# A decoder layer on one core: evacuations of PSUM and experts' ReLUs go to the engine that the kernel's own planner has free first

## The chip, the core and the metric

The kernel runs on one core of a Trainium2 chip. A core has TensorE (PE, matrix multiplications into PSUM), VectorE (DVE), ScalarE (ACT), GpSimd (POOL) and SyncE (SP, which here issues the DMA transfers). The metric is the device time of one execution in microseconds, given as the median of several runs. One more execution was profiled; its own time stands beside its span below.

## The reference, cut to what matters

A decoder layer over 16 sequences of 512 positions with 256 channels, in fp32. Each of three parts is added to its input and normalized.

```python
# 1. linear attention, 16 heads of 16 channels, two key and value sets
q = x + x @ Wq + bq;  ks[k] = x + x @ Wk[k] + bk[k];  vs[k] = x + x @ Wv[k] + bv[k]
state = prod_k( einsum('bhnd,bhne->bhde', ks[k] / 32, vs[k] / 32) )
x = norm(x + (norm(q @ state) * ln_g + ln_b) @ Wo + bo)
# 2. cross-attention to 64 context rows per sequence, 16 heads of 64
sim = (x @ Wq.T) . (ctx @ Wk.T) * 64**-0.5, masked;  attn = softmax(sim)
x = norm(x + (attn @ v) @ Wout.T + b_out)
# 3. mixture of 8 experts, each taking the first 1024 tokens with a positive weight
w = softmax(x @ router_w.T + router_b)
x = norm(x + sum_e w[:, e] * relu(x @ experts_inter[e]) @ experts_out[e])   # for the tokens taken
```

The router's weights are positive, so each expert takes the first 1024 tokens, which are the first two sequences (the "head"). A loop at the end of the program covers other cases; with these inputs it runs no pass.

## The kernel before

**Tiles and stages.** Rows of a sequence lie in four tiles of 128 (t = 0 to 3). Every result of TensorE goes into one of eight PSUM banks (`bank`, tag "ps", 128 x 512 fp32) and from there, through VectorE or ScalarE, to SBUF. The linear attention is folded: `gram` forms x^T x of a sequence (ps_g, ps_gt), `self_attention` multiplies it by the key and value weights (ps_gk, ps_s), builds a 256 x 256 matrix m (ps_m, ps_b) and applies it (ps_o), normalizes (z), transposes (ps_zt) and applies Wo (ps_p). The setup transposes the context and its weights (`context_keys`, `transposed`: tiles cn, nat to cT, wT), multiplies them (`context_rows`: ps_kv into st or stk) and, in `context_values`, multiplies the values by Wout (ps_vo into the four vst buffers) and stores them to DRAM (vo_dram), from where each sequence loads its vo tiles (six buffers). `router_columns`, `router_weights` and `output_weights` have small matmuls of 8 columns (L404 ps_rw, L537 ps_wo).

`cross_attention` forms the similarities of one row tile in two halves (ps_sim, L814); VectorE takes the maximum (mx, L820) and subtracts it (s, L821), ScalarE takes the exponential (L822). `softmax` then sums (sm, L800), inverts (L801), multiplies on GpSimd (L802) and transposes on VectorE into pT (L804). After the fourth row tile ps_x (L834, 256 records of 32 rows) multiplies pT and vo, and VectorE adds the result to x1 (L841). `routing` computes the expert weights (w_all) of a sequence. `experts` multiplies the head by an expert's first weights (ps_h, L946), takes the ReLU of each 128 x 256 piece into hT (L952 on ScalarE for odd f, L954 on VectorE for even f) and multiplies by the second (ps_e, L963; result added on VectorE, L970). `ranks` (L891 to L919) computes how many tokens come first for each expert, and `last_norm` writes the head out (y).

**Who evacuates.** `evac` (L186 on ScalarE, L188 on VectorE) copies a bank to SBUF, taking the two engines in turn through `flip`. It serves cT, wT, xT, st, stk, vst, g and xwoutT. Other evacuations have a fixed engine.

**What sets the order.** The program is written as six generators (streams): grams, context, self-attention, cross-attention, routing and experts. `weave` traces them step by step: it takes, of the streams that are ready at the planner's TensorE clock, the one that is least far in its plan (`Stream.time`), and lets it run to its next `yield`. A class `Model` follows the traced instructions with durations of its own: it holds when each engine is free (`free`), when each tile was made and last used, the end of the step (`end`) and TensorE's time in it (`took`). `yield WAIT` makes a stream ready only at the modelled end of its step, and `until(lambda: made(...))` polls until the model has a tile ready; in front of ps_x it polls for pT and vo. `beside` starts a further stream (each `softmax`, the loads of vo, each `last_norm`) that is ready at `model.end`. `in_order` then fixes the traced order on TensorE, VectorE, ScalarE and GpSimd; SP's transfers keep an order that the framework derives. So a change in the model's times changes the order on every engine.

Of the kernel before, what the change touches and what calls it, by code (L numbers as in the profile page):

```python
# [27 lines left out]
class Model:  # L28
# [2 lines left out]
    WIDE = {"PE": 0.25, "DVE": 0.15, "Activation": 0.15, "Pool": 0.15}  # L31

    def __init__(self, nc):
        self.nc, self.free, self.dma = nc, {}, 0.0
        self.made, self.used, self.slots, self.rows, self.seen = {}, {}, {}, P, 0

    def tile(self, name, key, bufs):
# [28 lines left out]
    def run(self):  # L66

        traced = self.nc.cur_bb.bb.instructions
        end = now = self.free.get("PE", 0.0)
        self.took = 0.0  # L70
        for ins in traced[self.seen:]:
            kind, engine = type(ins).__name__, str(ins.engine).split(".")[-1]
            aps = [[a.bass_ap for a in l if hasattr(a, "bass_ap")] for l in (ins.ins, ins.outs)]
            names = [[a.name for a in l] for l in aps]
            at = 0.0
            for made, used, l in ((1, 0, names[0]), (1, 1, names[1])):
                for n in l:
                    if kind == "InstDMACopy" and self.made.get(n, (0, 0))[1] == "SP":
                        continue
                    for known, book in ((made, self.made), (used, self.used)):  # L80
                        if known and n in book:
                            t, by = book[n]
                            at = max(at, t + (self.WIDE.get(by, 0.0) if by != engine else 0.0))
            if kind == "InstDMACopy":
                size = 4 * min(a.size() for l in aps for a in l)
                start = max(at, self.dma if now < 40 else 0.0)
                self.dma = start + size / 220e3
                done = self.dma + 2.0
            elif names[1]:
                start = max(at, self.free.get(engine, 0.0))  # L90
                done = self.free[engine] = start + self.duration(ins, kind, engine)
                if engine == "PE":
                    self.took += done - start
                else:
                    end = max(end, done + 0.15)
            else:
                continue
            for n in names[0] + names[1]:
                self.used[n] = max(self.used.get(n, (0.0, None)), (done, engine), key=lambda p: p[0])
            for n in names[1]:  # L100
                self.made[n] = (done, engine)
        self.seen, self.end = len(traced), end
        return end
# [13 lines left out]
def decoder_layer(  # L117
# [25 lines left out]
    nc = tc.nc  # L143
# [23 lines left out]
    model = Model(nc)  # L167
# [9 lines left out]
    def bank(name):  # L177
        return psp.tile([P, 512], FP, tag="ps", name=name)

    flip = [0]  # L180

    def evac(dst, src):

        flip[0] ^= 1
        if flip[0]:
            nc.scalar.copy(dst, src)  # L186
        else:
            nc.vector.tensor_copy(dst, src)  # L188
# [83 lines left out]
    with ExitStack() as att:  # L272
# [649 lines left out]
        def last_norm(b, t):  # L922
            y = wk1.tile([P, C], FP, tag=("z", "xt")[t % 2], name="y")
            yield WAIT
            yield from normalized(y.unsqueeze(1), lambda _: x2_head[:, b, t, :C], 1)
            yield WAIT
            nc.sync.dma_start(out=out[b, t * P:(t + 1) * P, :], in_=y)

        def experts():

            wi = wo_ = None
            yield from until(lambda: 0 in head_T and made(head_T[0]))
            for e in range(E):
                if e == 0:
                    wi = load_inter(e)
                    wo_ = load_outer(e)
                for n in range(CAP // TB):
                    b, t0 = divmod(n * TB // P, NT)  # L940
                    yield from until(lambda: b in head_T and made(head_T[b]))
                    hT = []
                    for f in range(NF):
                        ps = bank("ps_h")
                        for cc in range(NC):
                            nc.tensor.matmul(  # L946
                                ps[:, :TB], wi[:, cc, f * P:(f + 1) * P],
                                head_T[b][:, cc, t0 * P:t0 * P + TB], start=(cc == 0), stop=(cc == NC - 1),
                            )
                        h = ffn.tile([P, TB], FP, tag="hT", name="hT", bufs=12)  # L950
                        if f % 2:
                            nc.scalar.activation(h, ps[:, :TB], AF.Relu)  # L952
                        else:
                            nc.vector.tensor_relu(h, ps[:, :TB])  # L954
                        hT.append(h)
                        yield
                    if n == CAP // TB - 1 and e + 1 < E:
                        wi = load_inter(e + 1)
                    yield from until(lambda: finished["routing"] > b)
                    for t in range(TB // P):  # L960
                        ps = bank("ps_e")
                        for f in range(NF):
                            nc.tensor.matmul(  # L963
                                ps[:, :C], hT[f][:, t * P:(t + 1) * P], wo_[:, f, :],
                                start=(f == 0), stop=(f == NF - 1),
                            )
                            if f % 4 == 3:
                                yield
                        acc = x2_head[:, b, t0 + t, :C]
                        nc.vector.scalar_tensor_tensor(  # L970
                            acc, ps[:, :C], w_all[:, b * NT + t0 + t, e:e + 1], acc, ALU.mult, ALU.add
                        )
                        if e == E - 1:
                            beside(experts_st, last_norm(b, t0 + t))
                    if n == CAP // TB - 1 and e + 1 < E:
                        wo_ = load_outer(e + 1)

        def load_inter(e):
            t = ffn.tile([P, NC, FF], FP, tag="wi", name="wi", bufs=1)
            nc.sync.dma_start(out=t, in_=w_inter[e].rearrange("(c p) f -> p c f", p=P))  # L980
            return t

        def load_outer(e):
            t = ffn.tile([P, NF, C], FP, tag="wo_", name="wo_", bufs=1)
            nc.sync.dma_start(out=t, in_=w_out[e].rearrange("(f p) c -> p f c", p=P))
            return t
# [17 lines left out]
        def beside(st, gen):  # L1004

            new = Stream(gen).plan(st.time(), 0.0, 1.0)
            new.ready = model.end
            streams.append(new)

        def weave():  # L1010
            model.run()
            while streams:
                clock = model.free["PE"] = model.free.get("PE", 0.0)
                now = [st for st in streams if st.ready <= clock]
                if not now:
                    model.free["PE"] = min(st.ready for st in streams)
                    continue
                st = min(now, key=Stream.time)
                wait = next(st.gen, "end")
                st.end = max(st.end, model.run())  # L1020
                st.spent += model.took
                if wait == "end":
                    streams.remove(st)
                elif wait == WAIT:
                    st.ready = st.end
                else:
                    st.ready = clock + (wait or 0.0)
# [18 lines left out]
        def made(*tiles):  # L1046
            return all(model.made[t.name][0] <= model.free["PE"] for t in tiles)

        def until(ready):
            while not ready():  # L1050
                yield 0.5
# [63 lines left out]
        self_st, cross_st = Stream(all_self_attention()), Stream(all_cross_attention())  # L1115
        routing_st = Stream(all_routing()).plan(SETUP + STEP, STEP, 1.0)
        experts_st = Stream(experts()).plan(SETUP + 1.3 * STEP, (B - 0.1) * STEP, FFN)
        self_st.plan(0.0, SETUP, 16.5)
        cross_st.plan(SETUP, STEP, 28.0)
        traced = nc.cur_bb.bb.instructions  # L1120
        first = len(traced)
        streams += [grams_st, context_st, self_st, cross_st, routing_st, experts_st]
        weave()
        in_order(traced[first:])

# [86 lines left out]
```

## Time and profile before

| | |
|---|---|
| median of 3 runs | 1387.06 us (1386.35 to 1387.56) |
| the profiled execution: own time | 1389.4 us |
| the profiled execution: span | 1387.6 us |
| granted TensorE clock, mean | 0.994 |
| busy: TensorE, VectorE, ScalarE, GpSimd | 1365.9, 850.7, 402.2, 203.7 us |

The span runs from the first to the last instruction of the core; the execution's own time lies around it. Busy times are sums over instructions. In a row of a group, "x128" is the count, then come the busy time, the mean of one in ns, and the time that the engine stood idle before it with what ended that (the releaser). PEclk is the share of full speed that TensorE's clock was granted. A matmul in fp32 leaves two records, a transpose two; "ps_x x256" is one sequence.

### The profile page before, as it was taken

The numbers are of one execution on the slowest core, as the hardware profiler recorded it, in microseconds if no ns is written. First come the engines' busy times: TensorE is split into PE (matmuls) and PEld (weight loads), VectorE is DVE, ScalarE is ACT, GpSimd is POOL, SyncE is SP. The second block draws the span as 40 slices with busy tenths as digits, with TensorE's granted clock in tenths as the row PEclk, the third lists the DMA queues.
The fourth block names the chain that finished last, engine by engine and source line by source line (L and its number), as shares of the span: only waits on it lengthen the run. The fifth ranks groups of instructions, "written<-read, shape, count | busy, mean of one in ns | idle before, by whom it ended". The sixth has DMA issues, their size and how long they took to land.

```text
span 1387.6 us, 24209 instructions
## 1 busy us (share of the span) xinstructions
PE 1365.9 (98%) x9630; PEld 1077.9 (78%) x9630; DVE 850.7 (61%) x1957; ACT 402.2 (29%) x912; POOL 203.7 (15%) x140
## 2 busy tenths in 40 slices
PE   8999999999999999999999999999999999999997
PEld 5766576877878787878878787878888787878686
DVE  2445848466584848475584848475665939484744
ACT  1134224132232314142233323142323323232322
POOL 0001112112020111112020112112020202111200
PEclk9999999999999999999999999999999999999999
DMA  8657775511515153522606053513334061505211
GB/s 260 203 136 191 189 195 163 142 32 42 145 53 150 46 142 106 127 77 52 181 24 164 31 142 106 126 62 77 110 95 123 16 187 46 147 26 126 91 56 40
DMA packets 98372, 153.57 MB, mean 111 GB/s; under 512 B 15560, under 2 KB 70096, under 8 KB 98256
## 3 DMA queue, kind: packets, MB, share of 16 engines
q1 hardware_dynamic: 98256, 151.98, 40.1%
q8 instruction: 78, 1.28, 0.4%
q14 instruction: 38, 0.31, 0.1%
HBM read 114.71 MB, written 37.22 MB: 109 GB/s over the span
## 4 chain that ended last, share of the span: by engine, by line
PE 89%; DVE 5%; DMA 2%; SPq 1%; ACT 1%; issue 1%; ACTq 0%; DVEq 0%
PE ps_x L834 16%; PE ps_sim L814 15%; PE ps_e L963 15%; PE ps_h L946 15%; PE ps_gk L629 4%; PE ps_p L711 4%; PE ps_o L687 3%; PE ps_kv L437 3%; PE ps_t L233 2%; PE ps_kq L751 2%; PE ps_vo L492 2%; PE ps_s L641 2%; PE ps_g L555 2%; PE ps_zt L700 1%; PE ps_m L670 1%; PE ps_g L560 1%
## 5 line engine op out<-in xcount | busy, mean ns | idle before, releaser
L946 PE MATMUL ps_h<-head_T,wi 128*128 128x256 f32 x1024 | 239.1, 379 | 0.0
L834 PE MATMUL ps_x<-vo,pT 32*128 32x264 f32 x4096 | 234.9, 384 | 3.9 <-DVE pT L804 3.7
L814 PE MATMUL ps_sim<-kq,x1T 128*128 128x512 f32 x512 | 235.0, 593 | 0.0
L834 PEld LDWEIGHTS ps_x<-vo,pT 32*128 32x128 f32 x4096 | 211.5, 186 | 26.1 <-issue 5.6
L946 PEld LDWEIGHTS ps_h<-head_T,wi 128*128 128x128 f32 x1024 | 193.4, 190 | 38.8 <-issue 13.0
L802 POOL TENSOR_TENSOR s<-s,sm 128x1024 f32<-128x1024 f32 x64 | 121.7, 1901 | 539.8 <-DVE sm L801 501.4
L841 DVE TENSOR_TENSOR x<-ps_x,x 128x264 f32<-128x264 f32 x64 | 23.2, 426 | 226.3 <-PE ps_x L834 226.3
L822 ACT ACTIVATE s<-s 128x512 f32<-128x512 f32 x128 | 80.7, 630 | 276.1 <-DVE s L821 276.0
L814 PEld LDWEIGHTS ps_sim<-kq,x1T 128*128 128x128 f32 x512 | 94.5, 190 | 83.2 <-issue 74.5
L820 DVE TENSOR_REDUCE mx<-ps_sim 128x8 f32<-128x512 f32 x128 | 86.1, 673 | 42.0 <-PE ps_sim L814 41.6
L821 DVE TENSOR_TENSOR s<-ps_sim,mx 128x512 f32<-128x512 f32 x128 | 88.5, 692 | 4.4
L725 POOL TENSOR_TENSOR x<-x,bout 128x1056 f32<-128x1056 f32 x16 | 38.7, 2420 | 320.7 <-ACT hT L952 172.6
L804 DVE STREAM_TRANSPOSE pT<-s 128x1024 f32<-128x1024 f32 x64 | 78.6, 1228 | 7.0 <-POOL s L802 7.0
L952 ACT ACTIVATE hT<-ps_h 128x256 f32<-128x256 f32 x128 | 46.9, 376 | 119.9 <-PE ps_h L946 119.8
L701 ACT ACTIVATE zT<-ps_zt,shift,gain 128x512 f32<-128x512 f32 x32 | 23.2, 775 | 189.5 <-PE ps_zt L700 189.5
L800 DVE TENSOR_REDUCE sm<-s 128x16 f32<-128x1024 f32 x64 | 77.1, 1204 | 0.4 <-ACT s L822 0.4
L261 ACT ACTIVATE rstd<-bn_mv,eps 128x4 f32<-128x4 f32 (+1 forms) x70 | 20.7, 295 | 159.5 <-DVE bn_mv L250 156.0
L267 ACT ACTIVATE x<-x,off,rstd 128x264 f32<-128x264 f32 (+1 forms) x112 | 58.3, 591 | 29.3 <-DVE off L265 29.3
L687 PE MATMUL ps_o<-m,xT 128*128 128x264 f32 x256 | 66.7, 387 | 0.0
L954 DVE TENSOR_SCALAR hT<-ps_h 128x256 f32<-128x256 f32 x128 | 52.2, 409 | 22.5 <-PE ps_h L946 22.3
L711 PE MATMUL ps_p<-wo,zT 128*128 128x264 f32 x256 | 63.1, 387 | 0.0
L629 PE MATMUL ps_gk<-wk,g 128*128 128x256 f32 x256 | 61.2, 382 | 0.0
(174 smaller groups left out, 1897.4 us busy)
## 6 DMA issues: line engine op xcount, KB each, us to landing
vo<-vo_dram SPq DMA_DIRECT2D x512, 132.0 KB, 4.2
vo_dram<-vst SPq DMA_DIRECT2D x128, 132.0 KB, 2.4
xt<-in_x_dram SPq DMA_DIRECT2D x16, 512.0 KB, 4.0
wi<-L_ffn_experts_inter_dram SPq DMA_DIRECT2D x8, 1024.0 KB, 5.3
gx<-in_x_dram SPq DMA_DIRECT2D x15, 512.0 KB, 4.2
x_rest<-x SPq DMA_DIRECT2D x14, 512.0 KB, 3.1
out_dram<-x SPq DMA_DIRECT2D x14, 512.0 KB, 2.9
kT<-k_dram SPq DMA_DIRECT2D x8, 512.0 KB, 3.3
```

Of the source, the lines that this page charges most:

```text
L629: nc.tensor.matmul(ps[:, :C], blk, wk[:, j, k, :], start=(j == 0), stop=(j == NC - 1))
L687: nc.tensor.matmul(ps[:, :CX], xT[:, cc, t * P:(t + 1) * P], m[:, cc, :], start=(cc == 0), stop=(cc == NC - 1))
L711: nc.tensor.matmul(ps[:, :CX], zT[:, cc, t * P:(t + 1) * P], wo[:, cc, :], start=(cc == 0), stop=(cc == NC - 1))
L802: nc.gpsimd.tensor_mul(s, s, sm.unsqueeze(2).to_broadcast([P, NH, J]))
L804: nc.vector.transpose(probsT[:, :, t, :], s.rearrange("p h (a j) -> p (h a) j", a=2))
L814: nc.tensor.matmul(ps, x1T[:, cc, t * P:(t + 1) * P], kq[:, cc, hf * 512:(hf + 1) * 512], start=(cc == 0), stop=(cc == NC - 1),)
L820: nc.vector.tensor_reduce(mx[:, hs], sim, AX.X, ALU.max)
L821: nc.vector.tensor_sub(s[:, hs, :], sim, mx[:, hs].unsqueeze(2).to_broadcast([P, 8, J]))
L822: nc.scalar.activation(s[:, hs, :], s[:, hs, :], AF.Exp, scale=SCALE)
L834: nc.tensor.matmul(ps[q][:, :CX], probsT[pq, blk].rearrange("p t i -> p (t i)"), vos[c][pq, i, :], start=(c == 0 and i == 0), stop=(c == 7 ...
L946: nc.tensor.matmul(ps[:, :TB], wi[:, cc, f * P:(f + 1) * P], head_T[b][:, cc, t0 * P:t0 * P + TB], start=(cc == 0), stop=(cc == NC - 1),)
L963: nc.tensor.matmul(ps[:, :C], hT[f][:, t * P:(t + 1) * P], wo_[:, f, :], start=(f == 0), stop=(f == NF - 1),)
```

## The change

`evac` and the ReLUs of `experts` no longer take turns. A new function `scalar_first` first lets the model follow what has been traced so far, then takes ScalarE if the model has it free no later than VectorE, where a time before TensorE's own clock counts as TensorE's clock. If both are free by then, ScalarE is taken. Since the model now runs in the middle of a step too, `took` and `end` are collected over a step and set to zero before each step in `weave`; before, each call of `run` began anew. With that `model.end` is zero when `beside` is called at the beginning of a step, where it used to be the end of the step traced before.

```diff
@@ class Model
-        self.nc, self.free, self.dma = nc, {}, 0.0
+        self.nc, self.free, self.dma, self.took, self.end = nc, {}, 0.0, 0.0, 0.0
@@ Model.run
-        end = now = self.free.get("PE", 0.0)
-        self.took = 0.0
+        now = self.free.get("PE", 0.0)
+        end = max(self.end, now)
@@ decoder_layer
-    flip = [0]
+    def scalar_first():
+
+
+        model.run()
+        pe, dve, act = (model.free.get(e, 0.0) for e in ("PE", "DVE", "Activation"))
+        return max(act, pe) <= max(dve, pe)
 
     def evac(dst, src):
 
-        flip[0] ^= 1
-        if flip[0]:
+        if scalar_first():
             nc.scalar.copy(dst, src)
         else:
             nc.vector.tensor_copy(dst, src)
@@ experts
-                        if f % 2:
+                        if scalar_first():
                             nc.scalar.activation(h, ps[:, :TB], AF.Relu)
                         else:
                             nc.vector.tensor_relu(h, ps[:, :TB])
@@ weave
                 st = min(now, key=Stream.time)
+                model.took = model.end = 0.0
                 wait = next(st.gen, "end")
```

## The prediction

> **What bounds the kernel now.** I read the page's busy times first, then its chain, then TensorE's waits, then the timeline at each place where TensorE stands.
>
> ```profile
> span 1387.6 us, 24209 instructions
> PE 1365.9 (98%) x9630; PEld 1077.9 (78%) x9630; DVE 850.7 (61%) x1957; ACT 402.2 (29%) x912; POOL 203.7 (15%) x140
> PEclk9999999999999999999999999999999999999999
> PE 89%; DVE 5%; DMA 2%; SPq 1%; ACT 1%; issue 1%; ACTq 0%; DVEq 0%
> ```
>
> TensorE (PE) is the bound: busy for 98%, and 89% of the chain. Both orders hold the same 5461 TensorE instructions, so its work is fixed. What can be won is where it stands (1387.6 - 1365.9 = 21.7 us) or runs slowly; what can be lost is a new stop. VectorE (DVE) at 61% and ScalarE (ACT) at 29% matter only where one of them ends last in front of TensorE. Those places:
>
> ```profile
> PE ps_x L834 <- DVE pT L804: 3.7, 2, 3.2
> PE ps_t L233 <- DMA nat<-in_L_xattn_Wkv_dram: 2.4, 1, 2.4
> PE ps_e L963 <- DVE hT L954: 1.8, 1, 1.8
> PE ps_vo L492 <- DVE u L570: 0.8, 1, 0.8
> PE ps_vo L492 <- ACT st L186: 0.7, 1, 0.7
> ```
>
> Columns: us in total, times, longest. Between 349 and 1349 us TensorE stands for hardly anything (156.00 of 156.00 us busy in each stretch but one): nothing is to be won there. The open places are the start, the setup up to 193 us, two ps_x (192 to 349 us) and the tail.
>
> The clock has its own cost. Windows of 3.4 us, last columns PEclk, DMA share, GB/s:
>
> ```profile
> 15.50:18.90 3.40, 3.40 (x16) 3.17 (x15) 1.02 (x2) 0.58 (x1) 0.10 (x1) 0.50 0.79 277
> 66.70:70.10 3.40, 3.40 (x15) 3.21 (x15) 2.18 (x3) 0.00 (x0) 0.00 (x0) 0.50 0.00 0
> 70.10:73.50 3.40, 3.40 (x12) 2.75 (x12) 0.00 (x0) 0.00 (x0) 0.00 (x0) 0.50 0.00 0
> 336.30:339.70 3.40, 2.88 (x28) 2.56 (x32) 0.37 (x1) 0.00 (x0) 1.54 (x1) 0.50 0.02 5
> ```
>
> Half speed for one window costs 1.7 us of work. Two windows follow an idle gap (13 to 15 us, 333.6 to 336.8 us); two follow no gap at all.
>
> **The change part by part.** The instruction orders of both programs show what moves. 37 operations go from VectorE to ScalarE: 20 ReLUs, 8 xT, 10 st, 6 stk, 2 cT, a wT and an xwoutT leave VectorE, while 3 vst and a net 8 g pieces come to it. At the means of the groups (ReLU 409 against 376 ns, a 128x512 copy 683 to 692 against 574 to 595) VectorE loses about 25 us of 850.7, ScalarE gains about 22 us of 402.2. Neither is the bound, so this alone is worth nothing. More comes from the planner: it resets model.end before each step, so a softmax put beside the cross-attention is ready at once, where before it waited for the end of the step before. Between the second subtraction (L821) and the row sum (L800) stood mostly 5 to 11 VectorE instructions; now mostly 2 to 5. The whole TensorE order shifts with it.
>
> *1. Start: +1.85 us.*
>
> ```profile
> 9.81 1.04 PE L233 MATMUL ps_t<-ident,cn 128*128 128x128 f32 x8
> 10.69 0.27 PE L573 MATMUL ps_gt<-ident,g 128*128 128x128 f32 x1
> 10.79 1.91 PE L555 MATMUL ps_g<-gx 128*128 128x257 f32 x8
> 15.12 1.70 PE L233 MATMUL ps_t<-ident,nat 128*128 128x128 f32 x8 [2.42 <-DMA nat<-in_L_xattn_Wkv_dram]
> ```
>
> Before, ps_gt and the second sequence's ps_g fill the wait for nat. Now the transposes of nat stand ahead of both (all four cT copies go to ScalarE, and ps_gt waits for g behind them). The load is the eleventh row of SP's queue in both orders, so it lands at about 15.1 us as before. TensorE then stands from 10.7 on, and 0.11 + 1.74 us (8 at 0.2175, the steady pace of ps_g) are done later. The half-speed window is there already. Ends: 0 if nat lands earlier, +1.85; I take +1.85.
>
> *2. Clock at 63 to 74 us: -0.9.* The row first: PEclk is 0.50 from 66.7 to 73.5 us though TensorE never stands; what it did before was 16 matmuls of 8 columns (1.7 us), 8 transposes, and more 8-column ones. The Trainium skill, "TensorE: Matmul & The Clock Gate", Part 1 (the HAM clock gate), has the clock halved after an idle window of some 3.4 us and speaks of no narrow matmuls. By that rule these two windows should not exist and the order could change nothing: 0. By the row 3.4 us are at stake. The new order puts 8 wide ps_g records between L404 and the ps_wo block, but leaves narrow, transposes, narrow, so one slow window can remain, or both. Ends -3.4 and 0 (as now); I take -0.9, nearer to 0, since where a window falls is not visible in an order.
>
> *3. Setup, 104 to 193 us: -1.0.* A group of 16 ps_vo records takes 1.98 us undisturbed. Its results go through four vst buffers and 8 stores on SP, 0.58 us each (4.7 us a group). From 172.8 to 188.3 us three groups and the first record of ps_x lose 5.1 us (0.83 + 0.43, 0.93 + 0.83, 0.86, 1.28 over their usual pace). They stand 2 to 3 us of TensorE work apart, straight ahead of the first ps_x. In the new order ps_x (14.45 us) lies between them. But SP now has 30 loads of vo before the next stores; at 17.29 us for 32 of them, SP is free some 5 us after ps_x ends, and the second group after it needs its buffers about 2 us too early, the third likewise: up to 3 us back. And two halves of a vst tile on one engine take 0.8 us where two engines took 0.43: another 1.1 us. Sum -5.1 + 3 + 1.1 = -1.0; ends -5.1 (no stop returns) and +3 (the old ones stay, the new come).
>
> *4. The transposes ahead of ps_x: +2.4.* ps_x needs the fourth pT. In TensorE order I add up the work between the last ps_sim and ps_x ("cover"), and in VectorE order what it must do in that time. For the third sequence, before:
>
> ```profile
> 325.64 0.68 DVE L820 TENSOR_REDUCE mx<-ps_sim 128x8 f32<-128x512 f32 x1
> 331.83 1.21 DVE L800 TENSOR_REDUCE sm<-s 128x16 f32<-128x1024 f32 x1
> 335.43 1.25 DVE L804 STREAM_TRANSPOSE pT<-s 128x1024 f32<-128x1024 f32 x1
> 336.82 15.93 PE L834 MATMUL ps_x<-vo,pT 32*128 32x264 f32 x256 [3.25 <-DVE pT L804]
> ```
>
> Paces from this stretch: mx and subtraction 1.33 us, one z with its statistics 1.01, pT 1.14 (the last 1.25), row sum and reciprocal 1.41, three w_all 0.53, a ReLU 0.41. New order, counted from the end of the last ps_sim, with VectorE free 0.2 us after it (the shortest lag of before, 241.79 after 241.58) and 0.14 us to ps_x:
> second sequence: 0.2 + 1.33 + 1.01 + 0.41 + 1.14 + 1.41 + 3.03 + 0.53 + 1.25 + 0.14 = 10.45, cover 8.80: wait 1.65 (was 0.49).
> third: 0.2 + 1.33 + 0.41 + 1.14 + 1.01 + 1.41 + 2.02 + 0.53 + 0.2 + 1.25 + 0.14 = 9.64, cover 6.23: wait 3.4 (was 3.25); the slow window stays.
> The same sum gives 8.9 against 8.76 for the twelfth and 9.8 against 9.62 for the fourteenth, and 8.5 to 9.3 against 9.5 to 11.3 for most others; I put 1.1 us on all these. Together 1.65 + 3.4 + 1.1 - 3.74 = +2.4. Ends: 0 (VectorE, with less to do, runs ahead) and +9.8 (rival A with a slow window).
>
> *5. Tail: -1.75.* The ps_e at 1362.92 us waits 1.75 us for the ReLU that VectorE does after the chain of ranks (L898 to L919). In the new order no ReLU stands behind the end of that chain: the fifth is done after its 256-column steps, three are ScalarE's. Against it speaks the Trainium skill, "PSUM — Partial Sum Buffer", Engine vs sequencer instructions: ScalarE's and VectorE's queues are strictly first in, first out. The row: ScalarE stood 14.62 us before y at 1340.34 us with a ReLU behind. Here three ReLUs stand behind a y that waits for an off in VectorE's chain. From the start of ps_tot, off comes at 1.1 + 6.15 + 0.15 = 7.4 us (1353.44 to 1359.6 us in the trace for the same steps), y ends at 8.0, the ReLUs at 8.4, 8.8 and 9.2; ps_e, begun at 6.9, asks for them at 9.1, 9.5 and 9.9. So it just holds: without the rule nothing waits, with it 0.7 us are left. Ends -1.75 and 0.
>
> **Sum.** 1.85 - 0.9 - 1.0 + 2.4 - 1.75 = +0.6 us on the profiled execution, whose own time is 1389.4 us (span 1387.6). The median of the three timed runs is 1387.06, 2.3 us less; I put the difference on that: 1387.7. About 0.2% (2.8 us) is what a measurement can tell from no change.
>
> **The rivals.** *A, slower: VectorE reaches the last mx late.* In the trace its lag after the last ps_sim is 0.2 to 1.3 us; at 1.1 us everywhere step 4 gives 2.55 + 4.3 + 0.2 + 0.65 + 1.05 + 1.05 - 3.74 = +6.1 instead of +2.4, and a wait of 2.5 us at the second sequence brings one more half-speed window (1.7). That is 1387.7 + 3.7 + 1.7 = 1393.1. It decides from a lag of about 1 us. For it: covers shrank by about 1.6 us, VectorE's work by about 1. Against it: VectorE has fewer instructions ahead of the last mx.
> *B, faster: the setup's stops go and don't return.* Step 3 at -5.1 and step 2 at -3.4 give 0.6 - 4.1 - 2.5 = -6.0, 1381.1 in full; half of it 1384. Taken as 1382. For it: ps_x parts the groups. Against it: SP's loads stand ahead of the stores.
> *C, the choice of engine decides nothing:* it is 37 short operations beside idle engines, and the order does all of it. Then the time is the forecast's too; it has no chance of its own.
>
> **How the numbers follow.** Forecast (within 2.8 us) 0.40, A 0.37, B 0.23. Its own range is 1384.3 to 1389.9. The steps that lose are near to certain (1, 4), those that win lean on places of windows and buffers (2, 3), so A is ahead of B. The range of 8 in 10 runs from 1380.5 (B nearly in full) to 1395.5 (A with step 3 at +1.4).
>
> **What would show it.** Right: idle before ps_t (nat) near 4.3 us, ps_x waiting 1.5 to 2.5 and 3 to 4.5 us at the second and third sequence, no wait of ps_e near the end. Wrong: waits of over 1 us at ps_x after 349 us (A), PEclk full from 60 to 80 us and ps_vo at 1.98 us throughout (B), or a new releaser in TensorE's waits that no step names.

## The result: 1396.90 us against 1387.06, slower by 0.7%

The changed kernel takes 1396.90 us (median of five runs, 1394.55 to 1398.46) where the kernel before takes 1387.06 in the five runs beside it (1386.35 to 1388.61): a ratio of 1.0072, 95% interval 1.0056 to 1.0087. The forecast was 1387.7 us with a range up to 1395.5. The page of the changed kernel, the rows that answer to those shown of before:

```profile
span 1396.5 us, 24134 instructions
PE 1365.9 (98%) x9630; PEld 1082.2 (77%) x9630; DVE 822.4 (59%) x1920; ACT 423.5 (30%) x949; POOL 204.1 (15%) x140
PEclk9999999998999999999999999999999999999999
PE 86%; DVE 9%; DMA 3%; SPq 1%; ACT 1%; issue 1%; POOL 0%; DVEq 0%; ACTq 0%
```

VectorE lost 28 us of work and ScalarE gained 21, close to the 25 and 22 that the prediction worked out. TensorE is busy for exactly as long as before, 1365.9 us. So the 8.9 us of span are, in sum, time in which TensorE stands: 30.6 us in place of 21.7, and VectorE's share of the chain went from 5% to 9%. TensorE's waits say where (us in total, times, longest):

```profile
PE ps_x L838 <- DVE ks L594: 5.2, 1, 5.2
PE ps_t L237 <- DMA nat<-in_L_xattn_Wkv_dram: 4.7, 1, 4.7
PE ps_p L715 <- DVE vst L192: 4.1, 1, 4.1
PE ps_x L838 <- DVE pT L808: 3.4, 4, 1.6
```

A row names as releaser the instruction that came last before TensorE went on, which need not be the one whose result is read: ps_x reads pT, which ended at 340.09 us, and ks is the short operation that began just before that. The first row is the third sequence's ps_x, forecast at 3.4 us. The second is the start, forecast near 4.3. The third is a stop that no step of the forecast names as such, and the fourth holds four further ps_x: the second sequence's 1.59 us (forecast 1.65), and 0.43, 0.25 and 1.12 us at the fourth, twelfth and fourteenth.

To see more than the stops, I took for each matmul (tile, operands, shape) its median pace over the kernels, and added up by stretch what TensorE's rows took beyond it. This "excess" holds stops and slow clock alike. Both kernels were profiled once more late in the study ("again"):

| stretch, us | before, again | after, again | difference in the two pairs | forecast |
|---|---|---|---|---|
| start, 0 to 22 | 7.4, 6.3 | 9.2, 10.1 | +1.8, +3.9 | +1.85 |
| clock, 60 to 85 | 3.7, 0.5 | 2.0, 0.3 | -1.7, -0.2 | -0.9 |
| setup, 85 to 155 | 6.9, 6.9 | 4.6, 4.6 | -2.3, -2.3 | |
| setup, 155 to 235 | 7.7, 7.6 | 13.6, 12.8 | +5.9, +5.2 | -1.0 with the row above |
| second ps_x, 235 to 262 | 0.7, 0.7 | 2.1, 2.1 | +1.4, +1.4 | +1.2 |
| third ps_x, 318 to 360 | 4.9, 6.4 | 8.2, 8.2 | +3.3, +1.8 | +0.15 |
| 360 to 1340 | 3.3, 3.2 | 5.7, 5.7 | +2.4, +2.4 | +1.1 |
| tail, 1340 to the end | 2.6, 2.6 | 0.0, 0.0 | -2.6, -2.6 | -1.75 |
| all | 37.1, 34.3 | 45.4, 43.9 | +8.3, +9.6 | +0.6 |

The stretches left out differ by 0.1 us at most. Up to the 0.1 us that rounding leaves, the differences add up to the move of TensorE's last row (its end is at 1389.55 against 1381.32 us in the first pair).

### The profile page after: what moved, and what is told of

Read it like the earlier page. It is cut to its first block, busy times and chain, and to the rows that moved or that the text cites. A ratio compares the mean times of both kernels' runs of the same rounds, so it can differ in the third digit from the quotient of the medians.

```text
span 1396.5 us, 24134 instructions
## 1 busy us (share of the span) xinstructions
PE 1365.9 (98%) x9630; PEld 1082.2 (77%) x9630; DVE 822.4 (59%) x1920; ACT 423.5 (30%) x949; POOL 204.1 (15%) x140
## 4 chain that ended last, share of the span: by engine, by line
PE 86%; DVE 9%; DMA 3%; SPq 1%; ACT 1%; issue 1%; POOL 0%; DVEq 0%; ACTq 0%
PE ps_x L838 16%; PE ps_e L967 15%; PE ps_h L950 14%; PE ps_sim L818 13%; PE ps_p L715 4%; PE ps_gk L633 4%; PE ps_kv L441 3%; PE ps_o L691 3%; PE ps_kq L755 2%; PE ps_t L237 2%; PE ps_g L559 2%; PE ps_s L645 2%; DVE pT L808 1%; PE ps_vo L496 1%; DVE s L825 1%; DVE sm L804 1%
## 5 line engine op out<-in xcount | busy, mean ns | idle before, releaser
L838 PE MATMUL ps_x<-vo,pT 32*128 32x264 f32 x4096 | 238.0, 387 | 9.4 <-DVE ks L594 5.2
L838 PEld LDWEIGHTS ps_x<-vo,pT 32*128 32x128 f32 x4096 | 217.0, 187 | 29.0 <-issue 7.9
L956 ACT ACTIVATE hT<-ps_h 128x256 f32<-128x256 f32 x148 | 54.9, 380 | 162.0 <-PE ps_h L950 161.8
L271 ACT ACTIVATE z<-z,off,rstd 128x256 f32<-128x256 f32 x64 | 33.2, 589 | 106.9 <-DVE off L269 105.1
L441 PE MATMUL ps_kv<-cT,wT 128*128 128x512 f32 x128 | 61.0, 611 | 0.0
L715 PEld LDWEIGHTS ps_p<-wo,zT 128*128 128x128 f32 x256 | 49.4, 195 | 13.3 <-DVE vst L192 4.9
```

What stands on the lines that cost most here:

```text
L271: nc.scalar.activation(dst[:, t, :], src(t), AF.Identity, bias=off[:, t:t + 1], scale=rstd[:, t:t + 1])
L441: nc.tensor.matmul(ps, wT[:, cc, r % 4 * P:(r % 4 + 1) * P], cT[:, cc, q * 512:(q + 1) * 512], start=(cc == 0), stop=(cc == NC - 1),)
L715: nc.tensor.matmul(ps[:, :CX], zT[:, cc, t * P:(t + 1) * P], wo[:, cc, :], start=(cc == 0), stop=(cc == NC - 1))
L838: nc.tensor.matmul(ps[q][:, :CX], probsT[pq, blk].rearrange("p t i -> p (t i)"), vos[c][pq, i, :], start=(c == 0 and i == 0), stop=(c == 7 ...
```

## The experiments

All times are medians; a ratio is to the kernel before, measured beside that kernel. In the code, "..." marks what is left out.

### The two halves of the change, apart

The diff chooses engines, and it resets model.end, which makes streams started by `beside` ready at once. Each half alone:

```diff
@@ engines only: the changed kernel with the old readiness
-            new.ready = model.end
+            new.ready = model.last
-                model.took = model.end = 0.0
+                model.last, model.took, model.end = model.end, 0.0, 0.0
@@ reset only: the kernel before, turns kept
-            new.ready = model.end
+            new.ready = 0.0
```

> The engine is chosen by the planner as in the changed kernel, but a stream put beside another is ready at the end of the step before, as it was. Theory R (the reset of model.end does most of the harm, through the order in which softmax is traced): the start keeps its +1.8 us (ps_gt still behind the transposes of nat), the second and third ps_x wait about 2.6 and 2.1 us (covers 8.0 and 8.0 us against VectorE work of 10.1 and 9.5 us), no ps_x waits after 349 us; 1387 to 1390 us. Theory E (the choice of engine does it): most of the loss stays, 1394 to 1397 us.

> Engines take turns as before; only the streams put beside others are ready at once. Theory R: the start is as before (no +1.8 us), the third ps_x waits 3 us or more with the clock at half behind it, the fourth and some later ones 0.5 to 1 us; 1391 to 1396 us. Theory E: 1386 to 1389 us.

Engines only: 1392.64 us, ratio 1.0043 (1.0029 to 1.0056). Reset only: 1419.75 us, ratio 1.0243 (1.022 to 1.0266). Neither theory holds. R put the harm on the reset, but the choice of engine without it costs 5.9 us; and the reset alone costs 33 us, of which the choice of engine gives 23 back. The halves don't add. On the prediction's rival C, that the order does all of it, this decides nothing, because the choice moves the order too: in "engines only" VectorE has just 6 operations fewer than before (1951 against 1957), but TensorE's order leaves the old one at 10.7 us. No run has the new engines in the old order.

With the reset alone, the excess from 100 to 235 us is 34.4 us against 14.1 before; most of the rest lies at 262 to 318 us (4.5 against 0.2) and in the tail (6.4 against 2.6). The copies into vst stand longer for their stores. From 95 to 270 us, first VectorE's row, then ScalarE's:

```profile
DVE vst L188 <- DMA vo_dram<-vst: 23.3, 19, 7.8
ACT vst L186 <- DMA vo_dram<-vst: 21.3, 18, 5.4
```

In the kernel before the same two rows are 12.8 and 14.2 us, in the changed one 13.9 and 12.8. TensorE then waits for what came out late (4.9 us for a vst, 3.3 for x, 3.0 for xT). That these stood behind the copies in their engine's queue is read off the rows, not tested by itself.

Engines only has the new start (9.7 us) and stops of 4.38 and 5.66 us at the second and third ps_x, where 2.6 and 2.1 were expected from covers and durations. Something made VectorE's chain some 2 and 3.5 us longer than its operations are. In its trace, a w_all ahead of the second pT takes 2.19 us in place of 0.19, beside a run of GpSimd:

```profile
246.93 2.34 POOL L709 TENSOR_TENSOR xt<-xt,bo 128x1024 f32<-128x1024 f32 x1
247.12 2.19 DVE L864 TENSOR_TENSOR w_all<-w_all,rm 128x32 f32<-128x32 f32 x1
```

Ahead of the third pT a w_all takes 1.82 us and an off 2.29 us in place of 0.12. Whether GpSimd is the cause is the next experiment.

### Why the third ps_x waits 5.2 us

The changed kernel at the third sequence, rows of GpSimd, VectorE and TensorE in order of time:

```profile
334.34 1.90 POOL L806 TENSOR_TENSOR s<-s,sm 128x1024 f32<-128x1024 f32 x1 [4.69 <-DVE sm L805]
335.05 0.40 DVE L694 TENSOR_TENSOR z<-ps_o,bq_state 128x264 f32<-128x264 f32 x1
336.35 2.34 POOL L709 TENSOR_TENSOR xt<-xt,bo 128x1024 f32<-128x1024 f32 x1
336.55 2.19 DVE L864 TENSOR_TENSOR w_all<-w_all,rm 128x32 f32<-128x32 f32 x1
338.86 1.23 DVE L808 STREAM_TRANSPOSE pT<-s 128x1024 f32<-128x1024 f32 x1
340.23 17.39 PE L838 MATMUL ps_x<-vo,pT 32*128 32x264 f32 x256 [5.19 <-DVE ks L594]
```

s is ready at 336.24 us, and pT stands two instructions behind the subtraction that follows. But this subtraction of 32 elements, 0.19 us elsewhere, takes 2.19 us and ends when GpSimd's addition does (336.35 + 2.34 = 338.69). Before it, z from PSUM took its usual 0.40 us beside GpSimd's multiplication. The test shortens the addition in one sequence, where it leaves out bo for all but 8 of the 256 channels; all orders stay as they are:

```diff
-            nc.gpsimd.tensor_add(xt[:, :, :C], xt[:, :, :C], ...)
+            cut = C if b != 3 else 8
+            nc.gpsimd.tensor_add(xt[:, :, :cut], xt[:, :, :cut], ...)
```

> The changed kernel, with GpSimd's addition of bo in the fourth sequence cut from 256 to 8 columns (the rest of bo is left out there), all orders the same. Theory P (VectorE's subtraction in w_all stands for 2 us because GpSimd's addition runs, and the last pT stands behind it): the subtraction at 336.5 us takes 0.2 us in place of 2.19, ps_x waits 3.2 us in place of 5.19, and with less idle time 0 to 1.7 us of slow clock go too; 1393 to 1395 us. Rival (it waits for something else, such as ScalarE or its own operands): the subtraction stays near 2 us and the time at 1396 to 1397 us.

1394.01 us, ratio 1.005 (1.0032 to 1.0069), where the changed kernel has 1.0072: some 3 us less. The same places:

```profile
336.25 0.25 POOL L711 TENSOR_TENSOR xt<-xt,bo 128x32 f32<-128x32 f32 x1
336.44 0.19 DVE L866 TENSOR_TENSOR w_all<-w_all,rm 128x32 f32<-128x32 f32 x1
336.75 1.24 DVE L810 STREAM_TRANSPOSE pT<-s 128x1024 f32<-128x1024 f32 x1
```

and its row among TensorE's waits:

```profile
PE ps_x L840 <- DVE ks L595: 3.2, 1, 3.2
```

The subtraction is back at 0.19 us, the stop at 3.2 us, and the excess of 318 to 360 us fell from 8.2 to 5.0: 2.0 us of stop and about 1 us of slow clock behind it. Theory P stands, with the size that it gave. The Trainium skill, "SBUF — State Buffer", section "Who interferes with whom", has the rule: VectorE and GpSimd share a port pair, an exclusive lock, and a VectorE instruction with two SBUF inputs contends with a GpSimd instruction that reads SBUF, while one with at most one SBUF input does not, outside VectorE's two-port modes. The rows agree: w_all and rm are both in SBUF, z's first operand is in PSUM; and w_all, begun 0.20 us behind the addition, stood until the addition's end.

The next run moves the addition out of that place, in all sequences:

```diff
             transposed(xT, xt)
+            nc.gpsimd.tensor_add(xt[:, :, :C], xt[:, :, :C], ...)
             yield WAIT
...
             nc.gpsimd.tensor_copy(xt[:, :, C:], z[:, :, C:])
-            nc.gpsimd.tensor_add(xt[:, :, :C], xt[:, :, :C], ...)
```

> The changed kernel with GpSimd's addition of bo to xt put directly behind the transposes of xt in all sequences, nothing left out; TensorE's order is the same but for a few places. Theory P (VectorE's operations with two SBUF inputs stand while GpSimd's addition runs): the third ps_x waits 3.2 us or less in place of 5.19; 1393 to 1395 us, as with the addition cut short. Rival (at its new place the addition stops VectorE as well, at a place that matters): 1396 us or more.

1405.95 us, ratio 1.0133 (1.0112 to 1.0153). P is right about the third ps_x, which waits 3.2 us, and the rival about the time: the addition stops VectorE elsewhere. It now stretches one of the two operations that make state (L665, L666) at 13 of the sixteen sequences; ahead of the fourth ps_x:

```profile
403.64 1.89 DVE L665 TENSOR_TENSOR state<-sk 128x256 f32<-128x256 f32 x1
405.21 2.53 POOL L669 TENSOR_TENSOR xt<-xt,bo 128x1024 f32<-128x1024 f32 x1
405.57 2.45 DVE L666 SCALAR_TENSOR_TENSOR state<-state,headmask 128x256 f32<-128x256 f32 x1
```

Undisturbed, L665 and L666 take 0.38 and 0.42 us. Here L666 stands for the addition; L665 stands for a softmax's multiplication on GpSimd that ends at 405.25 us, and at this sequence it took 1.89 us in the changed kernel too. m is made from state, and TensorE waits for it, 4.7 us where the changed kernel has 0.3:

```profile
PE ps_o L692 <- ACT m L679: 4.7, 3, 2.3
```

### Why ps_p waits for vst

The changed kernel's SP queue, with TensorE's and VectorE's rows:

```profile
189.41 9.75 SPq L785 DMA_DIRECT2D vo<-vo_dram  x18
199.88 11.19 SPq L501 DMA_DIRECT2D vo_dram<-vst  x16
205.64 0.43 DVE L192 COPY vst<-ps_vo 128x264 f32<-128x264 f32 x1 [8.04 <-DMA vo_dram<-vst]
206.13 5.44 PE L715 MATMUL ps_p<-wo,zT 128*128 128x264 f32 x16 [4.11 <-DVE vst L192]
```

The copy stands 8.04 us for a buffer whose store is issued only behind 30 loads of vo. ps_p does not read vst: the 16 records of ps_vo ahead of it, 8 results, fill all eight PSUM banks, and ps_p needs one of them back. Two experiments change that queue. The first gives the stores to ScalarE's queue, with the planner's model told that they are still SP's, so that the orders stay:

```diff
-                        nc.sync.dma_start(
+                        nc.scalar.dma_start(
                             out=vo_dram[(q * NG + g) * GB + bl, :, r * 2:(r + 1) * 2, :],
                             ...
```

> The changed kernel, with its 128 stores of vst issued from ScalarE's queue and no longer from SP's behind the loads of vo; the order of TensorE's, VectorE's and GpSimd's instructions is the same. Theory Q (the stores stand behind the loads in SP's queue): the 4.1 us wait of ps_p at 206 us and the slow clock behind it go, the excess of 192 to 215 us falls from 6.6 to under 2 us; 1391 to 1393 us. Rival B (the transfers themselves are the bound, the DMA engines are busy for 85 to 97% from 180 to 205 us): the wait moves to the loads of vo in front of or inside the first ps_x; gain under 2 us, or a loss.

1422.39 us, ratio 1.0257 (1.0236 to 1.0278). The stop of ps_p is gone, as Q has it, but the kernel is some 26 us slower than the changed one. Neither theory had seen why:

```profile
81.04 0.38 ACT L191 COPY vst<-ps_vo 128x264 f32<-128x264 f32 x1 [2.11 <-DVE vst L193]
81.45 1.10 ACTq L502 DMA_DIRECT2D vo_dram<-vst  x2
82.97 0.66 ACT L191 COPY vst<-ps_vo 128x264 f32<-128x264 f32 x2 [1.54 <-issue]
83.66 1.10 ACTq L502 DMA_DIRECT2D vo_dram<-vst  x2
```

An issue holds ScalarE's queue for 0.55 us, longer than the copy in front of it (0.38). 128 of them are 70 us of ScalarE in a setup of 230. TensorE's waits for ScalarE's vst, st and x come to 15 us, where the changed kernel has 0.9 for vst and st. The second experiment keeps SP and changes its order alone, by an order dependency of the loads of the second sequence on the last store:

```diff
...
+                elif names[0][0].startswith("vo_dram"):
+                    loads += 1
+                    if loads > 32 and store is not None:
+                        tc.add_manual_dep(ins, store.name, ...)
```

> The changed kernel with one edit in SP's queue alone: the loads of vo of the second sequence stand behind the last store of vst; the orders of the other engines are the same. Theory Q (the stores stand behind the loads): the 4.1 us wait of ps_p at 206 us and the clock lost behind it go, the excess of 192 to 215 us falls from 6.6 to under 2 us, the loads still land before the second ps_x at 256 us; 1391 to 1393 us. Rival B (the transfers are the bound, whatever their order): the stop stays or moves to the second ps_x; 1395 to 1398 us.

1401.19 us, ratio 1.01 (1.0081 to 1.0119). Q's mechanism is right: no stop of ps_p, 192 to 215 us at 2.1. The gain is not there, since what is queued behind the loads is late next, the first expert's weights (wi). SP's rows and TensorE's:

```profile
183.94 0.42 SPq L741 DMA_DIRECT2D m<-in_mask_BxS_bf_dram  x1
192.70 0.40 SPq L303 DMA_DIRECT2D gx<-in_x_dram  x1
211.70 15.07 SPq L785 DMA_DIRECT2D vo<-vo_dram  x24
226.90 0.39 SPq L984 DMA_DIRECT2D wi<-L_ffn_experts_inter_dram  x1
233.01 2.04 PE L950 MATMUL ps_h<-head_T,wi 128*128 128x256 f32 x4 [9.27 <-issue]
```

Issuing 24 loads takes 15.1 us here, and wi landed 5.9 us after its issue, at 232.8 us. In this setup one queue serves stores, loads and weights, and this order moved the wait from one to another. The rival of this experiment (the transfers are the bound) was right about the sum, wrong about the place, and it is not shown that the transfers are a bound: SP issued nothing from 184.4 to 192.7 us, while the loads were held back for the stores. An order that uses this gap was not tried.

### Evacuations alone, ReLUs alone

> The changed kernel with the ReLUs taking turns by f as before; evacuations and the reset as changed. If the choice for evacuations is what keeps the reset's harm small (the setup alone cost 20 us with the reset and turns), the setup is as in the changed kernel and only the tail (ReLUs behind the ranks) and some ps_x after 1000 us lose up to 6 us: 1397 to 1404 us. If the ReLUs are what keeps it small: 1412 to 1420 us.

> The choice for the ReLUs alone, without the reset: evacuations take turns, streams put beside others are ready at the end of the step before. Nothing in the first 230 us moves. If the ReLUs' choice is a gain by itself, the tail loses 1.4 of its 2.6 us excess (as with both choices and no reset) and the third ps_x waits 3 to 4 us as before: 1385 to 1386.5 us. If what it gave in the changed kernel (about 5.5 us) came only from mending the reset's order: 1387 us or more.

Evacuations chosen, with the reset, ReLUs by `f % 2`: 1402.44 us, ratio 1.011 (1.009 to 1.013). From 100 to 235 us its excess is 17.3 us, as in the changed kernel (17.7): the evacuations' choice is what mends the reset's setup. Its tail has 1.7 us of excess and 1300 to 1340 us 1.3, where the changed kernel has 0.1 together; between 700 and 1200 us it loses 2 us more. So with the reset and the evacuations' choice in place, the choice of the ReLUs is worth some 5 us (ratios 1.011 and 1.0072).

The ReLUs' choice alone, without the reset: 1387.89 us, ratio 1.0003 (0.9992 to 1.0014), no difference. The tail did gain 1.4 us (1.15 against 2.55), as expected, and the third ps_x took it back. It waits 5.7 us in place of 3.25 because two operations in front of its pT stood for two runs of GpSimd:

```profile
331.69 1.90 POOL L809 TENSOR_TENSOR s<-s,sm 128x1024 f32<-128x1024 f32 x1 [9.19 <-DVE w_all L865]
331.83 1.82 DVE L867 TENSOR_TENSOR w_all<-w_all,rm 128x32 f32<-128x32 f32 x1
333.70 2.34 POOL L712 TENSOR_TENSOR xt<-xt,bo 128x1024 f32<-128x1024 f32 x1
333.77 2.29 DVE L272 SCALAR_TENSOR_TENSOR off<-bn_mv,rstd 128x4 f32<-128x4 f32 x1
```

off, with two SBUF operands of four elements, takes 2.29 us for 0.12.

### The slow clock at 60 to 85 us

Here the 8-column matmuls are made wider; the same is done to those of ps_rw (left out):

```diff
-                            ps[:, i * E:(i + 1) * E], nato[:, oc, i * P:(i + 1) * P], m[:, oc, C:],
+                            ps[:, i * P:(i + 1) * P].rearrange("p (a e) -> p a e", e=E),
+                            nato[:, oc, i * P:(i + 1) * P], m[:, oc, C:].unsqueeze(1).to_broadcast([P, P // E, E]),
```

> The kernel before, with the 8-column matmuls of ps_rw (L404) and ps_wo (L537) widened to 128 columns by repeating their 8 columns 16 times; only 8 are read, all orders are the same, and a 128-column record takes 0.111 us against 0.107. Theory N (narrow matmuls let the clock fall with no idle gap): the two half-speed windows at 65 to 75 us go, the excess of 60 to 85 us falls from 3.6 to under 0.5 us; 1383 to 1384.5 us. Rival (the windows come from something else there, such as transposes or the weight loads): the windows stay and the time is that of before within 1 us.

> The last one with the 8-column matmuls of ps_rw and ps_wo widened to 128 columns as well. If both gains stand and add up: 1384 to 1385.5 us, faster than the kernel before by more than 0.1%. If the slow clock at 65 to 75 us meets only some executions, half of that or less: 1385.5 to 1387 us.

> The kernel before, profiled once more. If the slow clock at 65 to 75 us belongs to its order, the excess of 60 to 85 us is 3 us or more again; if it depends on where the clock's windows fall in an execution, it can be anything from 0.3 to 3.7 us.

> The changed kernel, profiled once more. What belongs to its order comes back within 0.2 us: the third ps_x waits 5.2 us, the second 1.6, the start 9.2 to 10.4 us of excess; the clock at 60 to 85 us and the stops of 155 to 215 us (12.4 us together) may share out otherwise, as they did with the short addition (11.5 us).

Wide: excess 0.3 us in place of 3.7 in its profile, but 1386.44 us in time, ratio 0.9992 (0.9982 to 1.0003), no difference that the runs can tell. ReLUs and wide together: 1386.68 us, ratio 1.0006 (0.9994 to 1.0019). The kernel before, profiled again, explains it. The window of 68.26 to 71.67 us in its first and in its second profile (PEclk is the third column from the end):

```profile
68.26:71.67 3.41, 3.41 (x11) 2.85 (x11) 0.62 (x2) 0.00 (x0) 0.00 (x0) 0.50 0.00 0
```

```profile
68.26:71.67 3.41, 3.41 (x28) 3.06 (x28) 0.88 (x2) 0.59 (x1) 0.00 (x0) 1.00 0.00 0
```

The same program runs this stretch at half speed in one execution and at full speed in another. In the old order, narrow, four profiles have 3.7, 0.5, 3.7 and 0.5 us of excess here (before, twice; ReLUs alone; reset only, whose order is the old one up to 149 us), in the new order (eight profiles of kernels with the changed evacuations and the narrow matmuls) 0.3 to 2.1. The Trainium skill, "TensorE: Matmul & The Clock Gate", Part 1, says that the window of the clock's gate runs freely, so that results vary between executions; the two rows agree, but that the window's place is what differs between them is not shown. Whether the narrow matmuls or the transposes between them (Part 4 of that page has it that transposes don't count as busy in the same way) bring it on stays open, and no run here parts them: both wide profiles were at full speed, but so were several narrow ones. No version beats the kernel before.

The second profile of the changed kernel brought back the third ps_x (5.2 us), the second, and the start. The stop of ps_p was 0.9 us there in place of 4.1, but the sum of 155 to 235 us was 12.8 in place of 13.6: behind the first ps_x the granted clock was 0.50 from 192 to 195 us, so that a ps_kv took 3.78 us in place of 1.98, and what TensorE lost there it did not wait for later.

## Why the prediction was wrong, step by step

**What bounds it** was right: TensorE's work did not change, and what was lost is stops and slow clock. What the 37 moved operations are worth in an unchanged order, which the prediction put at nothing, no run shows.

**Step 1, start**, was right in mechanism; +1.85 us was called its upper end and is too low for it. Over the eight profiles with the new start the excess is 9.92 us in the mean, over the six with the old one 7.25: +2.7. The term that failed is "the half-speed window is there already". The transposes of nat in the second profile of before and in the changed kernel:

```profile
15.69 1.09 PE L233 MATMUL ps_t<-ident,nat 128*128 128x128 f32 x8 [3.32 <-DMA nat<-in_L_xattn_Wkv_dram]
15.09 1.97 PE L237 MATMUL ps_t<-ident,nat 128*128 128x128 f32 x8 [4.69 <-DMA nat<-in_L_xattn_Wkv_dram]
```

With the old start the stop is 2.1 to 3.5 us, and in two of the six profiles the clock stays at 1.00 behind it. With the new start the stop is 4.1 to 5.2 us, and all eight profiles have 1.97 us here, half speed.

**Step 2, clock**: the -0.9 us stand for a windfall of the execution. One profile's window was read as a property of the order.

**Step 3, setup**, failed in sign. The term "SP is free some 5 us after ps_x ends, and the second group after it needs its buffers about 2 us too early" named the very stop that came, 4.1 us at ps_p. But it was priced at "up to 3 us back" against -5.1 us for old stops that would go. From 85 to 155 us 2.3 us did go; from 155 to 192 us nothing (5.8 us in both first profiles), for the first ps_x itself lost 3.4 us (1.3 before), 0.9 of it a wait for a load of vo; and 192 to 235 us brought 5.9. So of the -5.1 us only -2.3 came, at another place, and the new stop with the slow clock behind it cost about twice the 3 us. Forecast -1.0, measured +3.6 and +2.9.

**Step 4, ps_x**, missed by about as much: +2.4 forecast, +7.1 and +5.6 measured. The second sequence was right (1.65 forecast, 1.59 measured). For the third the term "three w_all 0.53" failed. The work between the last mx and pT was added up from undisturbed durations, and one of the three took 2.19 us; with the addition short the stop is 3.2 us, so the rest of the sum held. The stop is 1.94 us longer than before in both pairs; the rest of the +3.3 us in the first pair is slow clock behind the stop (ps_x 17.39 us, before 15.93 and then 17.44). The trace of before had the warning, right ahead of its pT:

```profile
333.50 1.90 POOL L802 TENSOR_TENSOR s<-s,sm 128x1024 f32<-128x1024 f32 x1 [8.42 <-DVE ks L590]
333.76 1.68 DVE L865 TENSOR_TENSOR w_all<-w_all,rm 128x32 f32<-128x32 f32 x1
```

There it cost nothing, for pT needs the result of that same GpSimd operation. In the new order w_all comes 2 us later against GpSimd and meets the operation behind it, which pT does not need. Nor was it alone: of the 118 off and w_all operations with two SBUF operands in the trace of before, 28 took 0.87 to 1.87 us where the others have a median of 0.18, and each of the 28 ends within 0.06 us of the end of a GpSimd operation beside it.

For the other sequences 1.1 us were forecast and 2.4 came, by rival A's mechanism (VectorE late at the last mx) at two places. In the changed kernel at the fourth sequence, where the row behind the last ps_sim begins at 410.28 us:

```profile
410.82 1.21 DVE L804 TENSOR_REDUCE sm<-s 128x16 f32<-128x1024 f32 x1
412.84 0.68 DVE L824 TENSOR_REDUCE mx<-ps_sim 128x8 f32<-128x512 f32 x1
421.59 14.52 PE L838 MATMUL ps_x<-vo,pT 32*128 32x264 f32 x256 [0.43 <-DVE pT L808]
```

The row sum of an earlier softmax and two ReLUs stand ahead of the last mx: a lag of 2.56 us, 2.18 at the fourteenth, where before none was over 1.3. Engines only, without the reset, has neither wait. A's argument against itself, fewer instructions ahead of the last mx, was wrong there. Rival A's time (1393.1) was the nearest of the three by luck: most of the loss came from elsewhere.

**Step 5, tail**: -1.75 forecast, -2.6 measured; the gain came in full, and no wait of ps_e is left.

**The rivals**: B was wrong, since the setup's stops came back at another place; C stays open, since the choice of engine and the order never moved apart.

## What to carry to other kernels

A sum over VectorE's queue from mean durations held here only where no GpSimd operation ran beside it: look up what GpSimd runs at that moment, and treat a VectorE operation with two SBUF operands as able to last as long as GpSimd's, however small it is. A stop that a trace shows hidden costs nothing only while the order stays as it is. One profile's slow-clock window is not a property of the program until a second profile shows it too.

## What the runs showed of the hardware that I had not expected

- A 4-element VectorE operation took 2.29 us in place of 0.12 and a 32-element one 2.19 in place of 0.19 beside a GpSimd addition of 2.34 us. An operation with one operand in PSUM kept its pace beside GpSimd (z, 0.40 us).
- A DMA issue of 132 KB from ScalarE held its queue for 0.55 us, longer than the 0.38 us of the copy in front of it.
- The same program ran the same stretch at a granted clock of 0.50 in one execution and of 1.00 in another, worth 3.2 us of 1387.
